# First block of a two-layer graph attention: products with diagonals for transposes, warm-up products, and earlier weight sums

## The chip, the cores and the metric

The kernel runs on 1 core of a Trainium2 chip. The metric is device time in microseconds, the median of several executions; the profile is one execution of the same program. The engines are called TensorE (PE in the profile, PEld for its weight loads), VectorE (DVE), ScalarE (ACT), GpSimd (POOL) and SyncE (SP, which here issues the DMAs).

## The reference

128 graphs of 64 nodes, 768 features, float32. Cut to what matters:

```python
h = jnp.maximum(_layernorm(x, axis=-1), 0.0)          # (x - mean) / sqrt(var + eps), then relu
for l in range(2):
    m_left  = einsum('bsh,oh->bso', h, W_left[l])
    m_right = einsum('bsh,oh->bso', h, W_right[l])
    # scores from h and m, masked softmax over neighbours, context, layer norm, relu -> h
x = x + h
```

## The kernel before

The tokens are worked on in 16 blocks of 512. For each, a left and a right projection (15 products each, after a scheme that trades products for sums of tokens and of weights), then the scores. The products take features on the partitions, so a block has to be normalized and turned, in four quarters of 128 tokens. A record is one entry of the profile: a float32 matrix product shows as two records, a transpose as one, and each has a weight load with it. A product of the scheme is a group of eight records; "fifth product" and the like below count these groups. The granted clock is the share of full speed at which TensorE runs. Later blocks are turned far ahead, beside other work. The first block can't be: TensorE has nothing to do until it is there. The code of its opening:

```python
# statistics of quarter q on VectorE, root on ScalarE, then:
nc.vector.reciprocal(rs[:, q0:q1], sd[:, q0:q1])
nc.vector.scalar_tensor_tensor(nb[...], mv[...], -1.0, rs[...], op0=ALU.mult, op1=ALU.mult)
nc.scalar.activation(xr[q], xr[q], AF.Relu, bias=nb[:, q:q + 1], scale=rs[:, q:q + 1])
# turn(n, q): 6 transposes per quarter into two PSUM banks, then the copies
nc.tensor.transpose(p[:, c * P:(c + 1) * P], xr[q][:, ...], KEEP["ident"])
(nc.vector.tensor_copy if n < 2 else nc.scalar.copy)(to, p[:, :3 * P]...)
```

VectorE then makes the sums of tokens and of left weights; `needs` says how many of them are issued after which product. The right weights are summed by GpSimd and VectorE at numbered places (`put(slot, ...)`) among the projections. The second block's rows are normalized by ScalarE, turned in pieces of 32 by VectorE, stored to HBM and loaded back in their final layout:

```python
put(24, lambda: hold(TS[1, 0, 0]["tf"][:, 0, :1]))   # GpSimd waits for the last token sum
put(25, *rs[:7]); put_all(31, rv[7:11])              # right-hand weight sums
...                                                  # cut: statistics of the second block from slot 15 on
for q in range(Q):
    todo.append(lambda q=q: nc.vector.transpose(xb[:, :, q, :], xr[q]...))
todo.append(store)                                   # followed by load_h of the same block
```

The softmax here doesn't subtract the row's maximum and nothing guards it: scores larger than these inputs give would overflow.

## Time and profile before

| | us |
|---|---|
| median of 3 runs (2755.5 to 2762.2) | 2760.3 |
| span of the profiled run | 2755.1 |
| TensorE busy | 2726.7 |
| start of left projection, its fifth product, right projection | 13.92, 23.27, 42.34 |
| second block: first and third product | 70.02, 79.13 |

The last two rows are starts of lines in the timeline of TensorE.

### The profile page before, as it was taken

The numbers are of one execution on the slowest core, as the hardware profiler recorded it, in microseconds if no ns is written. First come the engines' busy times: TensorE is split into PE (matmuls) and PEld (weight loads), VectorE is DVE, ScalarE is ACT, GpSimd is POOL, SyncE is SP. The second block draws the span as 40 slices with busy tenths as digits, with TensorE's granted clock in tenths as the row PEclk, the third lists the DMA queues.
The fourth block names the chain that finished last, engine by engine and source line by source line (L and its number), as shares of the span: only waits on it lengthen the run. The fifth ranks groups of instructions, "written<-read, shape, count | busy, mean of one in ns | idle before, by whom it ended". The sixth has DMA issues, their size and how long they took to land.

```text
span 2755.1 us, 46372 instructions
## 1 busy us (share of the span) xinstructions
PE 2726.7 (99%) x18712; PEld 2339.0 (85%) x18712; DVE 1349.0 (49%) x2268; ACT 850.0 (31%) x1612; POOL 1192.1 (43%) x935
## 2 busy tenths in 40 slices
PE   8999999999999999999999999999999999999998
PEld 7888888888888888888788888888888888888886
DVE  6455455545454333333335444444444335676667
ACT  3222223222221154444621211121122214444443
POOL 3432352224223555555522344223222325887885
PEclk9999999999999999999999999999999999999999
DMA  6534433343332333343555433443344204555655
GB/s 195 129 75 97 121 83 81 86 120 94 76 77 75 102 105 119 119 150 123 148 127 149 101 75 76 108 118 79 76 98 120 59 26 145 160 170 166 175 161 146
DMA packets 234072, 310.82 MB, mean 113 GB/s; under 512 B 54146, under 2 KB 184450, under 8 KB 225666
## 3 DMA queue, kind: packets, MB, share of 16 engines
q1 hardware_dynamic: 233698, 307.45, 41.7%
q8 instruction: 149, 2.44, 0.4%
q14 instruction: 65, 0.53, 0.1%
q10 hardware_dynamic: 160, 0.39, 0.0%
HBM read 202.91 MB, written 104.86 MB: 112 GB/s over the span
## 4 chain that ended last, share of the span: by engine, by line
PE 96%; DVE 1%; DMA 1%; ACT 1%; issue 0%; SPq 0%; DVEq 0%; ACTq 0%
PE X L426 23%; PE V L426 16%; PE X L830 12%; PE Y L426 12%; PE Z L426 8%; PE V L830 8%; PE Y L830 6%; PE aux L453 5%; PE Z L830 4%; PE aux L645 2%; PE aux L668 1%; PE Y L668 0%; ACT ht L272 0%; DMA w_r<-in_w_right_dram 0%; DMA ht<-h 0%
## 5 line engine op out<-in xcount | busy, mean ns | idle before, releaser
L155 POOL TENSOR_TENSOR ts<-ht 128x512 f32<-128x512 f32 x441 | 586.8, 1340 | 1223.1 <-DMA ht<-h 531.1
L200 ACT ACTIVATE m<-X 128x512 f32<-128x512 f32 (+1 forms) x256 | 151.6, 592 | 1086.4 <-PE X L426 570.7
L155 POOL TENSOR_TENSOR ts<-ht,ts 128x512 f32<-128x512 f32 x189 | 248.8, 1323 | 135.1 <-PE X L830 60.5
L155 DVE TENSOR_TENSOR m<-m,V 128x512 f32<-128x512 f32 (+1 forms) x256 | 173.3, 677 | 269.4 <-PE V L426 269.2
L155 DVE TENSOR_TENSOR m<-m,X 128x512 f32<-128x512 f32 (+1 forms) x256 | 162.9, 677 | 249.3 <-PE X L426 248.7
L830 PE MATMUL X<-w_n,ts 128*128 128x256 f32 x1024 | 244.3, 380 | 0.9 <-ACT hl L200 0.6
L426 PE MATMUL X<-ts,w_l 128*128 128x256 f32 x1024 | 242.7, 380 | 0.1
L426 PE MATMUL X<-ts,w_r 128*128 128x252 f32 (+1 forms) x1024 | 238.7, 376 | 0.0
L155 DVE TENSOR_TENSOR m<-m,Z 128x512 f32<-128x512 f32 (+1 forms) x128 | 87.5, 683 | 306.5 <-ACT m L200 246.9
L830 PEld LDWEIGHTS X<-w_n,ts 128*128 128x128 f32 x1024 | 191.4, 190 | 33.4 <-issue 3.7
L426 PEld LDWEIGHTS X<-ts,w_l 128*128 128x128 f32 x1024 | 191.9, 190 | 30.2 <-DVE m L155 2.7
L426 PEld LDWEIGHTS X<-ts,w_r 128*128 128x128 f32 x1024 | 191.9, 190 | 26.1
L272 ACT ACTIVATE ht<-ht,b_col,a_col 128x512 f32<-128x512 f32 x192 | 143.6, 804 | 149.3 <-DMA ht<-h 149.3
L830 PE MATMUL Y<-w_n,ts 128*128 128x256 f32 x768 | 182.5, 379 | 0.0
L426 PE MATMUL Y<-ts,w_l 128*128 128x256 f32 x768 | 181.5, 379 | 0.5 <-DVE w_l L155 0.5
L426 PE MATMUL Y<-ts,w_r 128*128 128x252 f32 (+1 forms) x768 | 179.2, 376 | 1.3 <-POOL w_r L155 1.3
L426 PEld LDWEIGHTS Y<-ts,w_l 128*128 128x128 f32 x768 | 145.8, 190 | 20.7 <-DVE w_l L155 0.9
L830 PEld LDWEIGHTS Y<-w_n,ts 128*128 128x128 f32 x768 | 145.8, 190 | 20.4 <-issue 0.6
L426 PEld LDWEIGHTS Y<-ts,w_r 128*128 128x128 f32 x768 | 145.8, 190 | 19.1 <-POOL w_r L155 1.7
L155 DVE TENSOR_TENSOR hl<-hl,V 128x512 f32<-128x512 f32 (+1 forms) x136 | 89.1, 655 | 129.7 <-PE V L830 112.4
L200 ACT ACTIVATE hl<-X 128x512 f32<-128x512 f32 (+1 forms) x136 | 78.3, 576 | 221.4 <-PE X L830 218.6
L796 POOL TENSOR_TENSOR z<-z,b 128x768 f32<-128x768 f32 x62 | 112.0, 1817 | 79.7 <-DVE z L793 79.7
(162 smaller groups left out, 4730.9 us busy)
## 6 DMA issues: line engine op xcount, KB each, us to landing
ht<-h SPq DMA_DIRECT2D x63, 1536.0 KB, 7.2
h<-xb SPq DMA_DIRECT2D x124, 384.0 KB, 6.1
z<-z SPq DMA_DIRECT2D x128, 192.0 KB, 3.1
x<-z SPq DMA_DIRECT2D x128, 192.0 KB, 8.6
x<-in_x_dram SPq DMA_DIRECT2D x120, 192.0 KB, 8.6
xr<-in_x_dram SPq DMA_DIRECT2D x120, 192.0 KB, 3.7
out_dram<-xr SPq DMA_DIRECT2D x120, 192.0 KB, 2.7
adj<-in_adj_dram SPq DMA_DIRECT2D x64, 128.0 KB, 2.8
```

Of the source, the lines that this page charges most:

```text
L155: (eng.tensor_add if sign == "+" else eng.tensor_sub)(o, a, b)
L200: nc.scalar.activation(to(o), p, AF.Copy, scale=1.0 if sign == "+" else -1.0)
L272: nc.scalar.activation(ht, ht, AF.Relu, bias=cols[1][:, c:c + 1], scale=cols[0][:, c:c + 1])
L426: nc.tensor.matmul(p[:, g], w[ORDER[i][0]][:, c, g * P:(g + 1) * P], b()[t][:, c, :].rearrange(bs, s=S)[:, :, :ns], start=(new and g == c ...
L453: nc.tensor.matmul(p[h * S + e:h * S + e + 32, q, e:e + 95], ht[:, c, b * S + e:b * S + e + 32], mb[:, e:e + 95], start=(c == 0), stop=(c ...
L645: nc.tensor.matmul(cx[k][i, m, :HH], at[j, q, :], hl[j, q, m * HH:(m + 1) * HH], start=True, stop=True)
L668: nc.tensor.matmul(parts[r, k][n][i], at[j, q, :], hl[j, q, cut], start=True, stop=True)
L796: nc.gpsimd.tensor_add(zs[k], zs[k], rows["b"])
L830: nc.tensor.matmul(p[:, n], b[t][:, c, r * P:(r + 1) * P], w[s][:, c, :], start=(i in FIRST and i not in PRELOAD and n == c == 0), stop=(c ...
```

## The change

Its intent: spare ScalarE's normalizing pass by letting TensorE scale and centre while it turns (x as weights against a diagonal of 1/sd, and -mean broadcast against the same diagonal); free VectorE of its copies; have TensorE at full clock by then; and bring the right-hand weight sums sooner, because TensorE waited for them.

```diff
-                nc.scalar.activation(xr[q], xr[q], AF.Relu, bias=nb[:, q:q + 1], scale=rs[:, q:q + 1])   # first block
+                    nc.vector.tensor_scalar_mul(nb[:, q:q + 1], mv[:, q, :1], -1.0)
+                    nc.vector.tensor_scalar_mul(diag[q], KEEP["ident"], rs[:, q:q + 1])
-                        nc.tensor.transpose(p[:, c * P:(c + 1) * P], xr[q][:, ...], KEEP["ident"])
+                        nc.tensor.matmul(to, xr[q][:, ...], diag[q], start=True, stop=False)
+                        nc.tensor.matmul(to, nb[:, q:q + 1].to_broadcast([P, P]), diag[q], start=False, stop=True)
-                    (nc.vector.tensor_copy if n < 2 else nc.scalar.copy)(...)
+                    nc.scalar.activation(to, ..., AF.Relu)
+        if (l, u) == (0, 1):
+            todo.extend(none * 4)              # second block's turn on VectorE four places later
+                p = ps_st.tile([P, 2 * TH], F32, name="V")
+                for _ in range(28):
+                    nc.tensor.matmul(p[:, :P], KEEP["ident"], KEEP["ident"], start=True, stop=True)
-                for f in ws[:2]:               # two left weight sums on GpSimd, now one
-                needs = ("t", "wt", "wt", "ttwww", "wwww", "w", "tw", "t", "ww", "ww", "", "t", "t", "t", "t")
+                needs = ("twwwtt", "ttwww", "wwww", "w", "tw", "t", "ww", "ww", "tt", "", "tt")
-                        put(24, hold); put(25, *rs[:7]); put_all(31, rv[7:11])
+                        put(22, hold); put(23, *rs[:7]); put_all(27, rv[7:11])
```

(Shortened: lines joined; the reordering of the statistics and of the issue of the left weight sums cut.)

More of the change, by code (lines that the diff above doesn't have):

```diff
@@ L323, in transpose_rows, with half, inverse @@
             else:
-                KEEP["nb"] = nb
-                dev, inv = zip(*(scale(q, q + 1) for q in range(Q)))
-                todo.extend([stats[START[0]], dev[START[0]]])
+                diag, st = [pool.tile([P, P], F32, name="dg", bufs=Q) for _ in range(Q)], {}
+                def half(q, n):
+                    if not n:
+                        st[q] = stat.tile([P, 2, 6], F32, name="st", bufs=2)
+                    nc.vector.bn_stats(st[q][:, n, :], xr[q][:, n * HH:(n + 1) * HH])
+                    if n:
+                        nc.vector.bn_aggr(mv[:, q, :], st[q])
+                        nc.scalar.activation(sd[:, q:q + 1], mv[:, q, 1:], AF.Sqrt, bias=eps_in)
+                        nc.vector.tensor_scalar_mul(nb[:, q:q + 1], mv[:, q, :1], -1.0)
+                def inverse(q):
+                    nc.vector.reciprocal(rs[:, q:q + 1], sd[:, q:q + 1])
+                    nc.vector.tensor_scalar_mul(diag[q], KEEP["ident"], rs[:, q:q + 1])
+                todo.extend([lambda n=n: half(START[0], n) for n in range(2)])
                 for q, after in zip(START, START[1:] + (None,)):
                     if after is not None:
-                        todo.append(stats[after])
-                    todo.append(inv[q])
+                        todo.append(lambda q=after: half(q, 0))
+                    todo.append(lambda q=q: inverse(q))
                     if after is not None:
-                        todo.append(dev[after])
-                    todo.append(norms[q])
+                        todo.append(lambda q=after: half(q, 1))
         if (l, u) == (0, 0):
@@ L346, in turn @@
                     for c in range(3):
-                        nc.tensor.transpose(p[:, c * P:(c + 1) * P],
-                                            xr[q][:, (3 * m + c) * P:(3 * m + c + 1) * P], KEEP["ident"])
+                        to = p[:, c * P:(c + 1) * P]
+                        nc.tensor.matmul(to, xr[q][:, (3 * m + c) * P:(3 * m + c + 1) * P], diag[q],
+                                         start=True, stop=False)
+                        nc.tensor.matmul(to, nb[:, q:q + 1].to_broadcast([P, P]), diag[q], start=False, stop=True)
                 for m, p in enumerate(banks):
@@ L351, in turn @@
                     to = to[:, q // 2, :, q % 2 * 2:q % 2 * 2 + 2, :]
-                    (nc.vector.tensor_copy if n < 2 else nc.scalar.copy)(
-                        to, p[:, :3 * P].rearrange("p (c a s) -> p c a s", c=3, a=2))
+                    nc.scalar.activation(to, p[:, :3 * P].rearrange("p (c a s) -> p c a s", c=3, a=2), AF.Relu)
             for n, q in enumerate(START):
@@ L517, in pass_one @@
                 ws, vs = sums_w(0, "l", nc.gpsimd), sums_w(0, "l", nc.vector)
-                hold(KEEP["nb"][:, START[-1]:START[-1] + 1])
-                for f in ws[:2]:
-                    f()
-                t, w = deque(sums_t((1, 0, 0), nc.vector)), deque(vs[2:])
-                needs = ("t", "wt", "wt", "ttwww", "wwww", "w", "tw", "t", "ww", "ww", "", "t", "t", "t", "t")
-                for i, what in enumerate(needs):
+                ws[0]()
+                t, w = deque(sums_t((1, 0, 0), nc.vector)), deque(vs[1:])
+                needs = ("twwwtt", "ttwww", "wwww", "w", "tw", "t", "ww", "ww", "tt", "", "tt")
+                for i, what in enumerate(needs, -1):
                     for f in [(t if c == "t" else w).popleft() for c in what]:
-                        if i < 3:
+                        if i < 0:
                             f()
                         else:
-                            just.setdefault(i - 3, []).append(f)
+                            just.setdefault(i, []).append(f)
                 assert not t and not w
@@ L544, in pass_one @@
                         rs, rv = sums_w(0, "r", nc.gpsimd), sums_w(0, "r", nc.vector)
-                        put(24, lambda: hold(TS[1, 0, 0]["tf"][:, 0, :1]))
-                        put(25, *rs[:7])
-                        put_all(31, rv[7:11])
+                        put(22, lambda: hold(TS[1, 0, 0]["tf"][:, 0, :1]))
+                        put(23, *rs[:7])
+                        put_all(27, rv[7:11])
                         put(35, *rs[11:14])
```

## The prediction

> **What bounds the kernel now.** I read the page's busy table first, then the waits of TensorE alone, then the groups by form, then the timeline of the first 80 us, because the change touches only the first block.
>
> ```profile
> PE 2726.7 (99%) x18712; PEld 2339.0 (85%) x18712; DVE 1349.0 (49%) x2268; ACT 850.0 (31%) x1612; POOL 1192.1 (43%) x935
> ...
> PE aux L347 <- ACT x L297: 8.9, 1, 8.9
> PE X L426 <- DVE w_l L155: 1.5, 1, 1.5
> PE Y L426 <- POOL w_r L155: 1.3, 1, 1.3
> ```
>
> TensorE is busy for 2726.7 of 2755.1 us, so whatever is done elsewhere, at most 28.4 us (1.0%) of idle time is there to be won. The longest piece is the 8.9 us before the first transpose; the tail after the last product (some 9 us) isn't touched; the two others belong to the first block, at its left and right projections. A gain over 2% is ruled out by this one line.
>
> The opening in the timeline (start, duration, engine, line, operation):
>
> ```profile
> 1.05 0.29 POOL masks.py:199 TENSOR_SCALAR_AFFINE_SELECT ident<-ident 128x128 f32<-128x128 f32 x1
> 3.74 1.02 DVE L235 BATCH_NORM_STATS2 st<-x 128x6 f32<-128x384 f32 x2 [1.69 <-DMA x<-in_x_dram]
> ...
> 8.89 2.79 PE L347 MATMUL aux<-ident,x 128*128 128x128 f32 x12 [8.89 <-ACT x L297]
> ...
> 13.92 1.96 PE L426 MATMUL X<-ts,w_l 128*128 128x256 f32 x8
> ...
> 14.60 0.69 DVE L155 TENSOR_TENSOR ts<-ht 128x512 f32<-128x512 f32 x1 [0.22 <-ACT ht L352]
> ...
> 20.27 3.46 DVE L155 TENSOR_TENSOR w_l<-w_l,w_l 128x512 f32<-128x512 f32 x5
> ...
> 23.27 1.97 PE X L426 x8
> ```
>
> The last line is from the chain of waits. 24 transposes fill TensorE from 8.89 to 14.05. The first product follows at once, but the fifth (23.27) waits for VectorE, which is never idle for more than 0.3 us from 10.45 on: it runs the sums of tokens and weights back to back. The sum at 14.60 (B3-B2, for the second product) is the first that needs the last transposed quarter. From it to the fifth product lie 13 VectorE operations: 8.67 us. After 23.27 TensorE runs without a gap to 42.34, the start of the right projection: 11 products of 1.73 us. So **the end of the transposes sets the end of the left projection**: 14.05, + 0.55 to the sum, + 8.67, + 19.07 = 42.34.
>
> The right projection and the second block:
>
> ```profile
> 48.92 1.97 PE L426 MATMUL Y<-ts,w_r 128*128 128x252 f32 x8 [1.32 <-POOL w_r L155]
> ...
> 50.34 5.24 SPq L366 DMA_DIRECT2D h<-xb  x4
> ...
> 61.38 0.35 SPq L265 DMA_DIRECT2D ht<-h  x1
> ...
> 68.57 2.50 POOL L155 TENSOR_TENSOR ts<-ht 128x512 f32<-128x512 f32 x2 [11.20 <-DMA ht<-h]
> ...
> 70.02 1.89 PE L426 MATMUL X<-ts,w_l 128*128 128x256 f32 x8
> ```
>
> Here 1.3 + 0.4 us are lost to right-hand weight sums that come late. But a second line of work ends at the same place: store of the second block's h at 50.34, load at 61.38, landing 68.57, GpSimd's first sum some 1.25 us later (half of 2.50), i.e. 69.8, and the second block's first product at 70.02. It has 0.2 us of slack. Removing the 1.7 us of waits thus wins only 0.2 us unless the store comes earlier too.
>
> The granted clock of the page is 1.0 throughout, but the groups by form say otherwise for the opening:
>
> ```profile
> L426 PE MATMUL X<-ts,w_l 128*128 128x256 f32 x1024 | 242.7, 380 | 0.1
> ...
> L347 PE MATMUL aux<-ident,x 128*128 128x128 f32 x12 | 2.8, 423 | 8.9 <-ACT x L297 8.9
> L347 PE MATMUL Z<-ident,x 128*128 128x128 f32 x3 | 0.8, 421 | 0.0
> L347 PE MATMUL V<-ident,x 128*128 128x128 f32 x3 | 0.7, 340 | 0.0
> ```
>
> A transpose of 128 columns takes longer (421 ns) than a product record of 256 columns (380 ns), and the three last ones (V) suddenly less. Transposes start every 0.213 us (Z follows Y by 0.64 us for 3), product records every 0.216 us for twice the columns. So the opening ran at half speed and the full clock came at about 13.7 us, 4.8 us after the first transpose.
>
> **What the Trainium skill says.** (1) "TensorE: Matmul & The Clock Gate", Part 1, The HAM clock gate: a cold array runs at 1.2 GHz and goes to 2.4 after a busy window of about 3.4 us that runs freely. The trace agrees (4.8 us, a factor of two in columns per us). (2) The same page, Part 4, PE-mode transpose, says that transposes don't count as busy for that clock; here the clock rose during nothing but transposes, so the trace differs. (3) The same page, LDWEIGHTS: a load takes columns / 1.2 ns, 107 ns for 128. The trace shows means of 190, 132 and 110 ns for 128, 64 and 32 columns: a slope of 0.83 ns per column, as said, over a fixed 83 ns that overlaps. (4) "FP8 and Floating Point Precision", TensorE Precision Notes: true FP32 takes four passes. The trace agrees: a product of 256 columns (four per group in the program, eight records) takes 2 x 0.216 us, 1.69 ns a column, four cycles at 2.4 GHz; a transpose is one record of two.
>
> **The change, part by part.**
>
> *Products with diagonals.* 24 transposes (one record each) become 24 products with x as weights and 24 with the broadcast -mean, 128 columns each, two records each: 96 records. Warm, a record of 128 columns takes half of 0.216: 0.108 us, and its weight load (107 ns) just fits beside it. 96 x 0.108 = 10.4 us, against 5.16 us for the cold transposes (8.89 to 14.05). Warm transposes would have taken half of that: the new form is four times the work.
>
> *Earlier start.* ScalarE's normalizing pass (1.0 us per quarter, 7.72 to 11.88) is gone. From the durations in the timeline: statistics 3.74 to 4.76, aggregate 0.21, root 0.29 on ScalarE while VectorE does half of the next quarter, reciprocal 0.11, diagonal about 0.2: the first diagonal at about 6.0, the others 1.65 us apart, the last at about 10.9. If TensorE were free and warm, it could run from 6.05 to 16.5.
>
> *Work ahead.* 28 products of 128 columns, 56 records, start when the identity is there: 1.05 + 0.29, so about 1.45. Cold they take 0.213 us each. If the clock rises c us after the start, they end at 1.45 + c + (56 - c/0.213) x 0.108 = 7.5 + 0.49c: 9.9 us with the 4.8 us of the trace (my choice; 9.2 to 10.8 for 3.4 to 6.8, one to two windows). That is after the first diagonal: the warm-up delays the real work by about 4 us, which queues behind it in order. The turn then ends at 9.9 + 10.4 = 20.3.
>
> *Copies by ScalarE.* Eight copies of 0.48 us; VectorE loses four of 0.51. They follow bank by bank behind TensorE; only the last lies on the path: B3-B2 starts about 0.75 us after the end of the turn (0.2 latency, 0.48 copy).
>
> *VectorE's order.* One weight sum (0.6 us) moves from behind B3-B2 to ahead of it, so 12 operations, 8.05 us, are left to the fifth product. The sums ahead of it (first token sum, three of weights: 2.7 us after the second quarter's copies at about 16.2) end near 19, so they don't bind. VectorE then waits 2 us for TensorE.
>
> *Left projection.* It ends at 20.3 + 0.75 + 8.05 + 19.07 = 48.2, against 42.34: **5.8 us later**.
>
> *Second sums sooner.* The right-hand sums on GpSimd start behind the last token sum, which now comes about 3 us earlier relative to the end of the left projection; the 1.7 us of waits should go. But the transposes of the second block move behind the right projection's second read-out: VectorE reaches them about 4.85 us after the start of the right projection and ends them 3.7 us later, so the store is issued 8.55 us after it, against 50.34 - 42.34 = 8.0 before. The path store, load, first sum is 70.02 - 50.34 = 19.7 us. So the second block starts 28.2 us after the right projection does, against 27.7: **0.5 us later**, with a wait of 2.7 us for h in place of those for the weights.
>
> *Sum.* +5.8 + 0.5 = +6.3 us on 2760.3: 2766.6. From the second block on nothing changes, TensorE has no gap, so the delay is carried to the end. I shade to 2765, for the rivals lean to less.
>
> **The rivals.** (a) *The gain as intended*: the turn begins at 6 us and the waits at both projections vanish. For it: the 8.9 us of idle time are real, and VectorE is relieved. Against it: the four-pass arithmetic; even with the warm-up ended in time, the turn ends at 16.5, 2.4 us later than now, and the fifth product with it. With the second block's store earlier than I think, it would be 2756 to 2761. (b) *Weight loads bind*: with 128 columns loads and products are level, 107 and 108 ns; the transposes show a 230 ns load. If a record took 0.13 us in place of 0.108, the warm-up would end at 10.5 and the turn at 23: 2769. If loads and products didn't overlap at all (0.21), the turn would end near 34: 2780. Against it: at 256 columns the loads hide fully. (c) *The delay is hidden*: weights arrive from HBM up to about 19 us, and if something landing late set the pace, a later turn would cost nothing. Against it: the fifth product waited for VectorE's queue, which had no idle time, not for data: 2760.
>
> **Range and chances.** The runs before spread by 7 us, and the median of a few moves by 2. My sum gives 2762 to 2770; (a) widens it below, (b) above: 2757 to 2772. 2% is 55 us, nine times the effect: faster 0.005, slower 0.01, the rest within.
>
> **What would show it.** In the changed profile: 56 records ahead of the first diagonal product, of about 0.21 us each and then half, ending near 10; 96 records ending near 20; VectorE idle about 2 us before B3-B2; the fifth product at about 29; right projection from about 48 without a wait; then a wait of 2 to 3 us of the second block's first product, behind GpSimd and the load of h. I am wrong if the first diagonal product starts near 6, if 24 of their records take much less than 2.6 us, or if the right projection starts before 43.

## The result, and the profile after

The changed kernel took 2764.9 us (2763.1 to 2766.7, 4 runs) against 2758.3 for the one before in its 4 runs by then (2755.5 to 2762.2). The ratio is 1.0023, with a 95% interval from 1.0006 to 1.0040. It is the same within 2%, and slower by about 6 us.

The busy line of the changed kernel's page:

```profile
PE 2743.2 (99%) x18840; PEld 2354.8 (85%) x18840; DVE 1348.9 (49%) x2269; ACT 848.8 (31%) x1612; POOL 1191.8 (43%) x933
```

TensorE has 128 records more (56 + 96 - 24) and is busy 16.5 us longer. The span is 9.8 us longer (2764.9 and 2755.1), so only 6.7 us of that work fell into time that was idle before. (The control below, the kernel before once more, has a span of 2758.2, so the 9.8 is good to some 3 us only.) Its longest waits over the whole span:

```profile
PE X L443 <- POOL ts L155: 3.0, 1, 3.0
PE aux L470 <- issue: 2.0, 6, 0.4
PE X L443 <- DVE w_l L155: 1.5, 1, 1.5
PE V L520 <- POOL ident masks.py:199: 1.4, 1, 1.4
```

The 8.9 us before the first transpose have become 1.4, and the wait for right-hand weights is gone. The wait for left weights (1.5) is unchanged, and a new one of 3.0 us, for GpSimd's token sums, has come. The groups by form of the opening:

```profile
L520 PE MATMUL V<-ident 128*128 128x128 f32 x56 | 9.2, 346 | 1.4 <-POOL ident masks.py:199 1.4
L362 PE MATMUL aux<-dg,x 128*128 128x128 f32 x24 | 4.6, 275 | 0.0
```

The 56 warm-up records have a mean of 346 ns, a mixture of cold and warm ones; the products with diagonals, 275 ns, are all warm. The timeline (start, duration, engine, line, operation):

```profile
1.40 9.24 PE L520 MATMUL V<-ident 128*128 128x128 f32 x56 [1.40 <-POOL ident masks.py:199]
...
6.01 0.29 DVE L339 TENSOR_SCALAR dg<-ident,rs 128x128 f32<-128x128 f32 x1
...
10.48 0.39 PE L362 MATMUL aux<-dg,x 128*128 128x128 f32 x2
...
21.20 1.89 PE L443 MATMUL X<-ts,w_l 128*128 128x256 f32 x8
...
21.93 0.69 DVE L155 TENSOR_TENSOR ts<-ht 128x512 f32<-128x512 f32 x1 [2.30 <-ACT ht L368]
...
30.13 1.97 PE L443 MATMUL X<-ht,w_l 128*128 128x256 f32 x8 [1.48 <-DVE w_l L155]
...
49.62 1.86 PE L443 MATMUL X<-ts,w_r 128*128 128x252 f32 x8
...
59.43 5.22 SPq L381 DMA_DIRECT2D h<-xb  x4
...
77.00 2.48 POOL L155 TENSOR_TENSOR ts<-ht 128x512 f32<-128x512 f32 x2 [15.94 <-DMA ht<-h]
...
78.31 3.31 PE L443 MATMUL X<-ts,w_l 128*128 128x256 f32 x8 [3.03 <-POOL ts L155]
...
87.75 1.89 PE L443 MATMUL X<-ts,w_l 128*128 128x256 f32 x8
```

The reader sees the first diagonal at 6.3, and its product not before 10.48, when the warm-up is through. The left projection starts at 21.20 in place of 13.92. VectorE, which was idle for only 0.22 us at this sum before, waits 2.30 us for the last copy; from there the same sums lead to the fifth product (30.13; 23.27 before) and the right projection (49.62; 42.34), 7.3 us later. Then the second block's store leaves 9.8 us behind the start of the right projection (8.0 before), and the first product of that block waits 3.03 us for it.

One thing was not foreseen. The eight records at 78.31 last 3.31 us in all; such a group takes 1.89 elsewhere. The stretches around it (from:to, length, busy time of each engine, granted clock, DMA):

```profile
49.62:75.30 25.68, 25.66 (x121) 22.53 (x119) 15.57 (x20) 4.48 (x8) 11.21 (x8) 1.00 0.46 121
75.30:78.31 3.01, 0.00 (x0) 0.00 (x0) 0.68 (x1) 0.00 (x0) 1.31 (x2) 1.00 1.02 246
78.31:82.24 3.93, 3.93 (x28) 2.84 (x32) 1.41 (x4) 0.00 (x0) 3.77 (x4) 0.57 1.03 215
82.24:87.75 5.51, 5.51 (x192) 5.16 (x181) 0.91 (x3) 0.60 (x1) 5.51 (x5) 1.00 0.34 59
```

After three idle microseconds the clock is halved 0.5 us after the work resumes: the trace's own clock records put it at 0.5 from 78.83 to 82.24. From the second block's first product to its second (the scores lie between) it takes 7.61 us (78.31 to 85.92), against 5.88 before: 1.73 us more. In return the kernel before lost about 1.3 us behind its scores, which the changed one doesn't (of that under e8 to e11). At the third product the changed kernel is 8.62 us behind (87.75 to 79.13).

### The profile page after: what moved, and what is told of

It is laid out like the page before. It is cut to its first block, busy times and chain, and to the rows that moved or that the text cites. A ratio compares the mean times of both kernels' runs of the same rounds, so it can differ in the third digit from the quotient of the medians.

```text
span 2764.9 us, 46625 instructions
## 1 busy us (share of the span) xinstructions
PE 2743.2 (99%) x18840; PEld 2354.8 (85%) x18840; DVE 1348.9 (49%) x2269; ACT 848.8 (31%) x1612; POOL 1191.8 (43%) x933
## 5 line engine op out<-in xcount | busy, mean ns | idle before, releaser
L443 PEld LDWEIGHTS Y<-ts,w_l 128*128 128x128 f32 x768 | 145.8, 190 | 20.3 <-DVE w_l L155 0.5
```

The costliest lines, as they stand in the source:

```text
L443: nc.tensor.matmul(p[:, g], w[ORDER[i][0]][:, c, g * P:(g + 1) * P], b()[t][:, c, :].rearrange(bs, s=S)[:, :, :ns], start=(new and g == c ...
```

## The experiments

The milestones of all runs, in us from the start of the span, all read from the starts in the timeline of TensorE; the last column is when the clock records show half clock during the second block:

| run | left projection | fifth product | right projection | block 2, first | block 2, third | half clock |
|---|---|---|---|---|---|---|
| before | 13.92 | 23.27 | 42.34 | 70.02 | 79.13 | none |
| e12, before again | 13.97 | 23.02 | 42.09 | 69.78 | 78.53 | none |
| changed | 21.20 | 30.13 | 49.62 | 78.31 | 87.75 | 78.83 |
| e1 no warm-up | 19.67 | 28.60 | 48.09 | 76.92 | 86.20 | 76.51 |
| e2 warm-up of 14 | 17.95 | 26.88 | 46.36 | 75.37 | 84.75 | 75.16 |
| e3 no centring | 15.26 | 24.48 | 43.95 | 72.95 | 82.37 | 74.21 |
| e4 transposes | 14.02 | 23.97 | 43.44 | 72.00 | 82.33 | 71.71 |
| e5 old second sums | 20.33 | 29.25 | 48.73 | 76.61 | 84.91 | none |
| e6 only second sums | 13.94 | 23.37 | 42.53 | 71.54 | 80.97 | 72.54 |
| e7 before + 18 warm-up | 13.61 | 22.66 | 41.73 | 69.40 | 80.84 | 78.51 |
| e8 attempt | 13.47 | 22.52 | 41.59 | 67.56 | 79.39 | 76.24 |
| e9 attempt, no warm-up | 13.79 | 22.83 | 41.90 | 67.87 | 76.61 | none |
| e10 attempt, wide warm-up | 13.93 | 22.98 | 42.05 | 68.01 | 77.69 | none |
| e11 before + 9 wide | 14.25 | 23.29 | 42.36 | 70.04 | 80.31 | none |

**e12, the control.** The kernel before, unchanged.

> The kernel before once more, as a control of what two profiles and two sets of times of one kernel differ by. The first product at 13.9, fifth at 23.3, right projection at 42.3, second block's first product at 70.0, all within 0.3 us of the first profile; the stall of 1.2 us behind the second block's scores again, if it is a matter of the instructions' place; later stalls of 0.3 to 1.5 us at other places, so that the end differs by 1 to 2 us. Ratio within 0.2% of one.

Two profiles of one kernel differ by up to 0.3 us up to the second block and by 0.6 at its third product. Behind that, short waits of TensorE fall at other places: its last product starts at 2744.1 in the first profile and at 2747.2 in the second, 3 us apart. The ratio was 1.0004 (0.9990 to 1.0017). So differences of a microsecond can be told at the milestones but not in the times.

**e1, no warm-up.**

```diff
-                for _ in range(28):
-                    nc.tensor.matmul(p[:, :P], KEEP["ident"], KEEP["ident"], start=True, stop=True)
```

> The changed kernel without its 28 warm-up products. Theory A (the warm-up and the four-pass products with diagonals stand in one queue on TensorE, and VectorE's chain of sums follows their end): the first diagonal product starts when its diagonal is there, at about 6.3 us in place of 10.48; its records run cold (0.213 us apart) until the clock rises some 3.4 to 6.8 us later, then 0.111 us apart, so the left projection starts at 18.5 to 20.2 (21.20 with the warm-up), the fifth product at 27.5 to 29.2 (30.13), the right projection at 47 to 48.7 (49.62): 1 to 2.7 us sooner than the changed kernel at the end. Theory B (the warm-up earns its place: a cold TensorE is what would cost): 96 records at 0.213 us, left projection not before 26, slower than the changed kernel by 5 us or more.

The first diagonal product came at 6.3, the clock rose at 11.66, and everything up to the second block is 1.4 to 1.6 us sooner than in the changed kernel: theory A. In the time the gain can't be told (2763.4; 1.0022, 1.0005 to 1.0038, against 1.0023 of the changed kernel). The warm-up does not earn its place, and theory B, for which the cold clock was the cost, falls: 96 records cold would have taken 20 us, but those that do useful work raise the clock themselves.

**e2, half of the warm-up.**

```diff
-                for _ in range(28):
+                for _ in range(14):
```

> The changed kernel with 14 warm-up products in place of 28. Theory A: the 28 records end at about 7.4 us in place of 10.48, just when the clock rises; the diagonal products run warm from there, 96 x 0.111 = 10.65 us, left projection at about 18.1 (21.20), fifth product at 27.0 (30.13), right projection at 46.5 (49.62): 3 us sooner than the changed kernel, still some 4 us later than before (42.34). Theory C (a late turn is hidden behind weights that arrive or behind the second block's load): the right projection or the second block's first product (78.31) does not move.

The timeline of TensorE:

```profile
1.40 6.00 PE L520 MATMUL V<-ident 128*128 128x128 f32 x28 [1.40 <-POOL ident masks.py:199]
```

With 28 records in 6.0 us it ends as the clock rises (6.90). All milestones are 2.9 to 3.3 us sooner than in the changed kernel, as expected, and the right projection is still 4.0 us later than before: theory A, and theory C falls, for the shift is carried to the second block. The time was 2760.5 (1.0017, 1.0002 to 1.0032).

**e3, no centring products.** The mean is not subtracted, so the result is wrong.

```diff
-                        nc.tensor.matmul(to, xr[q][:, ...], diag[q], start=True, stop=False)
-                        nc.tensor.matmul(to, nb[...].to_broadcast([P, P]), diag[q], start=False, stop=True)
+                        nc.tensor.matmul(to, xr[q][:, ...], diag[q], start=True, stop=True)
```

> The changed kernel without the 24 centring products (wrong result on purpose: the mean is not subtracted). Theory A: 48 records of 0.111 us less, the left projection starts 5.3 us sooner, at 15.9 (21.20). The first token sum and three weight sums now reach to about 17.1 on VectorE and bind a little: fifth product at about 25.3 (30.13), right projection at 44.8 (49.62), 4.8 us sooner at the end. If weight loads set the pace of these records rather than the products, the step per record is not 0.111 and the 48 that are left take more than 5.3 us. Theory C: nothing moves at the second block.

The left projection started 5.9 us sooner. 48 records of 0.111 us are 5.3; the rest is the clock, which in this run rose at 5.95, 1.2 us sooner than in the changed kernel (7.15), and that alone is worth half of 1.2. The fifth product came 5.65 us sooner; the weight sums bind less than I had expected. The time was 2759.3 (1.0008, 0.9993 to 1.0023). So the half of the products that only centres costs over 5 us of the opening.

**e4, the old opening in the changed kernel.** Warm-up and sooner sums stay.

```diff
-   products with diagonals, copies by ScalarE            # in words
+   nc.scalar.activation(xr[q], xr[q], AF.Relu, bias=..., scale=...); nc.tensor.transpose(...); copies by both engines
```

> The changed kernel with the old opening: normalized by ScalarE, 24 transposes, half the copies on VectorE; the 28 warm-up products and the sooner second sums stay. Theory A: transposes start at 10.5 behind the warm-up, warm, 0.108 us each; the last waits for ScalarE's pass (11.9), so they end at about 13.1; VectorE has its four copies again and one weight sum more ahead of the sum that needs the last quarter, which starts at about 16 and binds: fifth product at about 24.3 (30.13 changed, 23.27 before), right projection at 43.8 (49.62; 42.34), the second block's first product at 72.5 (78.31; 70.02). In time 5 to 6 us under the changed kernel and 1 to 2 over the one before. If the products with diagonals are not the cost, it stays at the changed kernel's time.

By form, a warm transpose now has 273 ns in place of 423:

```profile
L349 PE MATMUL aux<-ident,x 128*128 128x128 f32 x12 | 1.5, 273 | 0.0
```

Twelve take 1.5 us in place of 2.8. The right projection starts at 43.44, 6.2 us sooner than in the changed kernel: the turn by products with diagonals is the cost. (The normalizing pass and the copies go back with it; what the copies alone are worth no run tells.) But the time was 2761.0 (1.0015, 1.0000 to 1.0030), some 4 us above the kernel before, where I had expected 1 to 2. The milestones say why: the opening loses only 1.1 us to the one before up to the right projection, 2.0 up to the second block, where TensorE waits 2.9 us for GpSimd's sums, and 3.2 up to its third product, for the clock drops there too and TensorE stands another 0.7 us in the scores. The second suspect, the sooner second sums, is in this run as well.

**e5, the old places of the second sums in the changed kernel.**

```diff
-        if (l, u) == (0, 1):
-            todo.extend(none * 4)
-                        put(22, hold); put(23, *rs[:7]); put_all(27, rv[7:11])
+                        put(24, hold); put(25, *rs[:7]); put_all(31, rv[7:11])
```

> The changed kernel with the places of the right-hand weight sums and of the second block's transposes as before (new opening, 28 warm-up products and order of token sums kept). Theory A (the sooner second sums push the second block's store later, and the idle time that this makes on TensorE also drops its clock to half for 3.4 us): the waits for right-hand weights come back (1 to 1.7 us), the store follows the start of the right projection by about 8.0 in place of 9.8 us, TensorE waits for the second block's h under 1 us in place of 3.0 and the clock stays at full: second block's first product at about 77.3 (78.31), its third at 85 to 86.4 (87.75), 1.4 to 2.7 us sooner. Theory D (the sooner sums gain what they were meant to): slower than the changed kernel by the 1.7 us of waits.

The timeline of TensorE in the right projection and at the second block:

```profile
53.83 1.86 PE L441 MATMUL Y<-ts,w_r 128*128 128x252 f32 x8
57.84 1.94 PE L441 MATMUL X<-ht,w_r 128*128 128x252 f32 x8 [2.15 <-DVE w_r L155]
...
76.61 1.89 PE L441 MATMUL X<-ts,w_l 128*128 128x256 f32 x8
```

The wait for right-hand weights is back, 2.15 us, and the one for h is gone; from the right projection to the second block it takes 27.88 us, against 28.69 with the sooner sums. The clock stays at full and the scores are passed in 5.88 us, not 7.61. The third product is 2.84 us sooner, 0.9 of it from the opening, where the clock rose at 5.33 and not at 7.15. That is theory A at the milestones. The time, 2762.7 (1.0027, 1.0013 to 1.0041), does not confirm it: it is as long as that of the changed kernel. The profiled runs differ at the last product by 3.3 us in the expected direction (2750.6 and 2753.8), but the control shows 3 us of that size without any change. What 2.8 us at the third product are worth in the time is left open.

**e6, only the second sums, in the kernel before.**

```diff
+        if (l, u) == (0, 1):
+            todo.extend(none * 4)
-                needs = (..., "ww", "ww", "", "t", "t", "t", "t")
+                needs = (..., "ww", "ww", "tt", "", "tt")
-                        put(24, hold); put(25, *rs[:7]); put_all(31, rv[7:11])
+                        put(22, hold); put(23, *rs[:7]); put_all(27, rv[7:11])
```

> The kernel before with only the sooner second sums (opening with transposes, no warm-up). Theory A: right projection at about 42.7 (42.34) without waits for weights, store some 9.8 us later (8.0), the second block's first product 28.6 us after the right projection, at 71.3 (70.02), behind a wait of 3 us for h; the clock drops to half for 3.4 us there, third product at about 81.5 to 82 (79.13). Slower than before by 2 to 3 us. Theory D: the second block starts 1.7 us sooner than before.

The waits of TensorE from 40 to 90 us are a single line:

```profile
PE X L428 <- POOL ts L155: 3.4, 1, 3.4
```

The waits for weights (1.3 and 0.4 before) are gone, and one of 3.4 us for the second block's h stands in their place, with half clock from 72.54. The second block begins 1.5 us later than before, its third product 1.8 later (2.4 against the control). Theory D falls. The time, 2758.4 (1.0011, 0.9998 to 1.0025), goes the same way without being clear of zero.

**e7, a warm-up alone, in the kernel before.**

```diff
+                for _ in range(18):
+                    nc.tensor.matmul(p[:, :P], KEEP["ident"], KEEP["ident"], start=True, stop=True)
```

> The kernel before with 18 warm-up products ahead of the transposes, nothing else. Theory A: the warm-up ends before the first normalized quarter is there (8.9), the transposes run at 0.108 us each as they become ready, the last about 12.5 in place of 14.05; ScalarE's four copies then bind, so the sum that needs the last quarter starts only some 0.6 us sooner: fifth product at 22.6 (23.27), right projection at 41.7 (42.34), second block at 69.4 (70.02). 0.6 us sooner, not to be told from zero in the times. Theory B (the clock is what costs): 2.6 us sooner.

Up to the second block as expected by theory A: 0.6 us sooner (0.4 than the control), although the turn ended 1.6 us sooner (12.49 and 14.05), so theory B falls; ScalarE and VectorE bind. The 0.6 itself is hardly clear of what profiles differ by: at the right projection e11, with a warm-up too, gains nothing, and e9, without one, is 0.4 sooner. But then the third product is 1.7 us later. The timeline of TensorE:

```profile
71.22 3.47 PE L453 MATMUL aux<-m,ht 128*32 128x95 f32 x160
77.07 0.86 PE L453 MATMUL aux<-m,ht 128*32 128x95 f32 x32 [2.37 <-issue]
77.86 3.19 PE L426 MATMUL Z<-ts,w_l 128*128 128x256 f32 x8
```

TensorE stands for 2.37 us behind 160 of the 192 score records without a wait that the profile shows ("issue"), and then the clock drops (3.19 us for eight records). The expectation had nothing of this. The time was 2758.4 (1.0010, 0.9995 to 1.0025).

**e8, an attempt at a better kernel.** If two lines meet at the second block, both must come sooner: the weights as in the change, and the second block's statistics four places sooner.

```diff
+                18 warm-up products, as in e7
+                put(22, hold); put(23, *rs[:7]); put_all(27, rv[7:11])
-                needs = (..., "ww", "ww", "", "t", "t", "t", "t")
+                needs = (..., "ww", "ww", "t", "t", "tt")
-                    slot = 14 if l else 15
+                    slot = 14 if l else 11
```

> An attempt at a better kernel: the kernel before with 18 warm-up products, the sooner right-hand sums, and the second block's statistics four places sooner on ScalarE so that its store leaves earlier instead of later. Theory A (two lines meet at the second block, weights and h, and both must come sooner): right projection at about 41.7 (42.34), no waits for weights, store about 4.5 to 6 us after it (8.0), second block's first product at 67.4 to 68 (70.02) without a wait, third about 7.7 us later, at 75.5 (79.13): 2 to 3.5 us sooner than before. If ScalarE's earlier work holds up VectorE and the read-outs, the left projection grows by 1 to 2 us and the gain is lost.

The second block starts at 67.56, 2.5 us sooner than before and without a wait, as expected. Then the gain is lost: 2.30 us of standing behind 161 score records, and half clock from 76.24:

```profile
75.22 0.86 PE L453 MATMUL aux<-m,ht 128*32 128x95 f32 x31 [2.30 <-issue]
```

The third product is at 79.39, where the kernel before is. The time was 2757.0 (1.0007, 0.9994 to 1.0019).

**e9, the attempt without a warm-up; e10, with half the instructions in it; e11, e7 with half the instructions.** The new theory, F, was that TensorE waits for its own instructions: a 16 KB transfer of the queue that the page calls "instruction" runs at just this time. The warm-up is meant to be as long in e10 and e11 as in e8 and e7 (5.99 and 5.65 us; 5.78 and 6.86), but in 9 products of 256 columns:

```diff
-                for _ in range(18):
-                    nc.tensor.matmul(p[:, :P], KEEP["ident"], KEEP["ident"], ...)
+                for _ in range(9):                        # e10, e11; none in e9
+                    nc.tensor.matmul(p[:, :2 * P]..., KEEP["ident"], KEEP["ident"]...to_broadcast([P, 2, P]), ...)
```

> The attempt of e8_ahead without its 18 warm-up products (same instructions on TensorE as the kernel before). Theory A: right projection at about 42.3, the second block's first product at 68.2 to 68.5 (70.02 before, 67.56 in e8). Theory F (the stall of 2.3 us inside the second block's score products in e7 and e8 is TensorE waiting for its own instructions: 72 more of them put the end of what is fetched into the densest stretch, and the clock drops after it): without the warm-up the stall falls where it does in the kernel before, in the product after the scores, 1.2 us, and the clock stays at full; third product of the second block at about 77.4 (79.13 before, 79.39 in e8), 1.7 us sooner than before. Theory G (the stall comes of data that isn't there or of the warm-up itself): 2.3 us again and a clock drop.

> The attempt of e8_ahead with its warm-up in half the instructions: 9 products of 256 columns in place of 18 of 128 (36 more instructions on TensorE than before in place of 72), as long in time. Theory A: second block's first product at 67.6, as in e8. Theory F: the stall moves 36 instructions later than in e8, to the end of the score products or just behind them, and is shorter than 2.3 us; third product at 76.5 to 78 (79.39 in e8). Theory G: as e8.

> As e7_warm18, with 9 products of 256 columns in place of 18 of 128: the same warm-up in time, half its instructions. Theory A: second block's first product at 69.4 as in e7. Theory F: the stall in the scores (2.4 us in e7, at 74.7) comes 36 instructions, some 0.4 us, later in the scores or behind them, and is shorter, and the clock may stay at full: third product 0.5 to 2.5 us sooner than e7's 80.84. Theory G: as e7.

The lines of TensorE's timeline at which the standing ends, first the kernel before, then the control, e9, e10 and e11:

```profile
78.06 1.24 PE L426 MATMUL Z<-ts,w_l 128*128 128x256 f32 x5 [1.25 <-issue]
```
```profile
77.45 1.24 PE L426 MATMUL Z<-ts,w_l 128*128 128x256 f32 x5 [0.88 <-issue]
```
```profile
75.65 1.13 PE L426 MATMUL Z<-ts,w_l 128*128 128x256 f32 x4 [0.77 <-issue]
```
```profile
75.41 0.53 PE L453 MATMUL aux<-m,ht 128*32 128x95 f32 x13 [1.64 <-issue]
```
```profile
78.02 0.53 PE L453 MATMUL aux<-m,ht 128*32 128x95 f32 x14 [2.22 <-issue]
```

The count at the end tells the place. Without a warm-up 3 or 4 records behind the scores had run. With 36 instructions more (18 products and their loads) it stops at 178 or 179 of the 192 scores, some 17 records sooner; with 72 more, at 160 or 161, some 35 sooner. Each record has a load with it, so that is 36 and 72 instructions to within two: the place goes with the instruction count, not with the data or the time, and theory G falls. I had the direction of e10 right and its start as well, but the gaps of 1.64 and 2.22 show that the length varies. In all seven runs with this gap (before, control, e7 to e11) the work resumes 1.25 to 1.5 us after the 16 KB transfer has ended (in e8: transfer 72.67 to 73.85, work again at 75.22); the shorter gaps of e4 (0.65 us) and e5 (0.32 us) end 1.34 and 1.19 us after one. Counted from the start of the span, TensorE had started 935 to 938 records and loads when it stopped in these seven runs, and 939 in e4. In e5, whose kernel has 256 of them more than the kernel before, it was 1190, again 3 records behind the scores. The page of the kernel before gives the queue for the whole span (transfers, MB, share):

```profile
q8 instruction: 149, 2.44, 0.4%
```

These are 149 transfers of 16 KB for 37,424 records and loads, 251 each; the changed kernel has 150 for 37,680. That such a transfer brings TensorE's instructions is inferred from these counts, the queue's name and the time, and no run shows it directly.

e9 and e10 keep the full clock and reach the third product 2.5 and 1.4 us sooner than the kernel before (1.9 and 0.8 than the control). Their times were 2753.7 and 2753.5, against 2756.0 for the kernel before in the same rounds: 0.9994 (0.9982 to 1.0007) and 0.9995 (0.9982 to 1.0007). That is 2 us less by the medians and not clear of zero. Against the changed kernel's 1.0023 they are the best versions that were run. e11 took 2757.0 (1.0005, 0.9989 to 1.0020); its third product came only 0.5 us before that of e7, though its clock stayed at full, for it stood almost as long, and its opening was 0.6 later than that of e7. That is not the warm-up, which ended 1.8 us before the first transpose: VectorE waited 1.01 us for rows of x to land, which it did not in e7.

## Why the prediction was right

The predicted time was met (2765 and 2764.9), and the steps can be checked one by one. Its own sum was +6.3 us; the ratio of 1.0023 is 6.3 us on 2758, with an interval of 1.7 to 11. So the agreement of the totals is closer than the times can show, and closer than the steps deserve. The 2765 was also met by two slips that cancel: it is counted from 2760.3, 2 us above the median of the same kernel when the result came (2758.3), and it was shaded down by 1.6 from the sum.

| step | predicted | measured |
|---|---|---|
| full clock after the first product | 4.8 us | 5.75 (at 7.15) |
| end of the warm-up | 9.9 | 10.48 |
| 96 records of the turn | 10.4 | 10.72 (0.112 each) |
| left projection starts | 20.3 | 21.20 |
| from there to the sum that needs the last quarter | 0.75 | 0.73 |
| from that sum to the fifth product | 8.05 | 8.20 |
| fifth product to right projection | 19.07 | 19.49 |
| right projection later than before by | 5.8 | 7.28 |
| right projection to the second block's store | 8.55 | 9.81 |
| store to the second block's first product | 19.7 | 18.88 |
| right projection to second block | 28.2 | 28.69 |
| wait for h | 2.7 | 3.03 |

- **What bounds the opening** was right: the end of the turn set the fifth product by VectorE's chain of sums. e1 to e4 moved the left projection over 7 us, and the fifth product and the right projection followed to within about 1 us each time. In e4 the chain itself bound, as expected. In the kernel before, though, the end of the turn and VectorE's own queue are nearly level, which the prediction's "sets" hides: in the control the turn ends 1.05 us sooner (13.00 and 14.05), the fifth product comes 0.25 sooner. The tail behind the last product, "some 9 us" in the prediction, is 10.6 us, which changes nothing in the sum.
- **The four-pass arithmetic** was right. e4 shows it from the other side: with transposes the right projection starts 6.2 us sooner in the same warm-up.
- **The warm-up delays the work behind it**: right, 10.48 for a diagonal ready at 6.3. The clock's rise came later than in the trace before, which is the larger part of the 0.6 us. Rival (a), the gain as intended, fell with that line. Rival (b) had a trace of truth: 0.112 in place of 0.108 us per record, 0.3 us in all.
- **The left projection** lost 0.3 us more than predicted at 40.88, at a wait for VectorE. The changed kernel and e1 to e5, which share its order of VectorE's sums, all show it, and the runs with the old order of the first sums show none or, in e6, a smaller one.
- **The sooner second sums lose rather than gain**: right in sign (e6: second block 1.5 us later) and in mechanism (wait for h in place of those for weights). Its size, 28.2 for 28.69, is two errors that nearly cancel. VectorE came to the second block's transposes 5.65 us after the start of the right projection and not 4.85, and needed 4.1 us for them and not 3.7; ahead of them stood four weight sums of 1.0 to 1.7 us each, where the shortest take 0.6 to 0.7 (why they differ is not shown). The way from the store to the first product was 0.8 us shorter than taken.
- **Two terms were missing.** The idle 3 us cost 1.7 more through the clock; and the 1.3 us behind the scores, which I read in the trace before as "issue" but left out of the sum, fell away. That TensorE had stood still beforehand, so that its instructions were there, is the likely reason and not shown; e5, with as many instructions and no such wait, stands 0.32 us at that place. The two terms nearly cancel. Rival (c), a hidden delay, fell: e2 and e3 carry their shift to the second block.

At the third product the profile shows +8.6, by milestones that repeat to 0.6 us; the times show +6.3 with 4 to 5 us on either side. That my sum hit the second number is partly luck.

## What to carry to other kernels

Before replacing transposes by products, count passes: here a float32 product of 128 columns costs two records where a transpose costs one, and centring doubles that again, so the idle time that was won was more than filled. A warm-up must end before the real work is ready, since it stands in the same queue. When a wait is removed where two lines meet, look at the slack of the other one first: the right-hand sums had 1.7 us to give, the load of h only 0.2 (0.6 in the control). The change also moved the store of that h 1.8 us later, and the idle time that came of it cost its length and then the clock.

## What the Trainium skill lacked or had wrong

- "TensorE: Matmul & The Clock Gate", Part 4, PE-mode transpose, says that transposes don't count as busy for the clock. In the kernel before, in the control and in e6 and e9 nothing but transposes ran, and the clock rose during or just after them (at 13.72, 11.91, 14.51 and 12.09 us, 3.4 to 5.7 us after the first).
- The same page, Part 1, asks for a busy window to rise and an idle one to fall, without saying how busy. In the 14 traces, cut into windows of 3.413 us from the clock's rise: it rose after windows that were 88 to 100% busy and not after ones of up to 68%. In the second block it fell after windows that were 8 to 42% busy, and held after one of 45% (e11); but at the end of the span it fell after windows of up to 49% too (46 in e7, 48 in e10, 49 in e12). So busy time alone gives no sharp threshold, and 2 us of idle time can be enough to lose the clock, if they fall into one window (e7).
- The same page gives spacings for bf16 only. A float32 product of 128 columns with a weight load each, warm, took two records of 0.112 us (96 records in 10.72 us); cold, two of 0.213. A transpose of 128 columns in float32 takes one record, 0.213 cold.
- "Runtime: NRT & Kernel Launch", Instruction fetch mechanics, tells of instructions that are fetched in blocks of 16 KiB, 256 instructions, and calls the cost of crossing such a border mostly hidden. If the inference above holds, it was not hidden here: TensorE stood 0.3 to 2.4 us in or behind a stretch of 192 records that start every 0.02 us, at a place that moved by 17 or 35 records when 36 or 72 instructions were put ahead of it. The queue's transfers fit the block (251 records and loads each).
- Belonging to no page, on reading the profile: the granted clock was printed as 1.00 in the opening, where transposes plainly ran at half speed; the clock records of the trace begin only with the first rise.
